# A fused transformer step on one core: three normalisations issued at other places or by another engine

## The chip, the cores and the metric

The kernel runs on 1 core of one Trainium2 chip. The metric is the device time of the program in microseconds; the time of a kernel is the median of its runs. Everything is computed in fp32.

In the profile the engines are PE (TensorE, matmuls), PEld (TensorE's weight loads), DVE (VectorE), ACT (ScalarE), POOL (GpSimd) and SP (SyncE, which only issues transfers here). Nearly all instructions are issued through a helper on line 50, so that "L50" says little; the names of the tiles, written as "out<-in", say which step a row is.

## What is computed

The input is a batch of 16 sequences `x` of 256 tokens by 256, and a context of 16 by 77 by 256. Four sublayers follow each other, each with a residual and a tanh gate:

```
x = x + tanh(g_xattn[0]) * attention0(ctx_1024, layernorm(x))   # 16 heads of 64, latents x attend to x and context
x = x + tanh(g_ffn[0])   * experts(layernorm(x))                # router softmax, best 2 of 8 experts per token
x = x + tanh(g_xattn[1]) * attention1(layernorm(x), ctx_1024)   # 16 heads of 16, 77 keys, mask, side factor
x = x + tanh(g_ffn[1])   * gated_linear_attention(layernorm(x))
```

In `attention0` the sequence is normalised twice: by the sublayer's own layer norm, and again inside. Each layer norm is `(x - mean) / sqrt(var + 1e-5)` over the 256 features of a token.

## The kernel before

The 16 batches are worked through stage by stage: stage 0 is the first attention, stage 1 the experts, stage 2 the second attention, stage 3 the gated linear attention. A token lies on a partition, so that a batch is 128 partitions by 2 rows of 256. The fast version of each stage (`stage0_fast`, `stage1_fast`, `stage2_fast`, `stage3_fast`) is the one that runs. A flag that is computed on the way would send the input through a slower version, which does not run here.

**What sets the order.** The engines run beside each other, each one through its own instructions in order, waiting on semaphores. Instructions issued through `dve`, `act`, `pool` and `pe` are kept in the order in which the program is written (line 160, class `Pinned`, line 42). Transfers through `nc.sync` (SP's queue) and `nc.gpsimd.memset` are not pinned; the framework orders those. Hand-written tables say which step of which batch is issued at which place.

**A layer norm** is made of three steps. `moments` (line 184) has DVE take the mean and variance of each token (tiles `bst`, `mv`). Then `rs` = 1/sqrt(var + eps) is computed either by POOL, with a multiply-add and a power (two instructions), or, with `by_act=True`, by ACT, with a logarithm and an exponential (two instructions). `normed` (line 200) multiplies -mean by `rs` on DVE (one instruction into `rs`) and then has ACT write the normalised rows (`y`, `xn`, `cn` or `rxn`), one activation per 256-wide row.

**Stage 0** works in 64 units, 16 batches by 4 groups of heads (loop at line 716). A unit issues the scores of four heads (`scores`, tile `sc`) with three exponentials on ACT (`e`), then on POOL the sums over keys (`sums`, tiles `es` and `esum`), then the values of the unit before (`values`, tiles `o`, `rd`), and the queries and keys of the next unit (`heads`, tile `qk`). Tables name what is issued ahead of a unit's scores (`ahead_of`, line 681), behind its scores (`behind_scores`, line 683) and behind its values, by the unit's group g. In them a batch's normalisation for the next batch is spread: statistics of `x` and context in group 3, `y` behind the scores of group 3, the second statistics ahead of the next group 0, and `normed_all`, which writes `xn` and `cn`, behind the scores of that group 0. In group 1 follow the transposes (`turn`), in group 2 the values' projection (`all_values`). The first batches are different: batch 0's norms stand in front of the loop, and batch 1's first three steps too (lines 711 to 713). Its second statistics and `normed_all(1)` come from the tables at unit 0.

In passing, stage 0 also routes batches for stage 1 (class `Route`, line 370 and after): norm, transposes, router logits, choice of two experts, weights, ranks, the places of the rows, and four scatters per batch, by which POOL writes weighted rows into DRAM (`rows`), sorted by expert. The last batches' routing steps lie in stage 1.

**Stage 1** runs 48 expert units (`units`, line 1125), two halves of 24, three units per expert and half (two, two and one tiles of 128 rows). In each round of the loop the next unit's transposes are issued first (`turned(u + 1)`, copied out by ACT into `xT`), then the unit's matmuls (`expert(u)`, tile `ex`, copied out by DVE into `y` and written to `rows_out` by SP), then the steps that the table `steps` (line 1110) has for this unit. The table places batch 15's routing (`last`): statistics in unit 1, norm in 2, and so on, to the four scatters in units 12 to 15. Expert rows are fetched by SP (`fetch`, tile `xin`). Rows of the second half need the last batch's scatters. Between the halves the context's keys and values for stage 2 are projected (`context`, tiles `k`, `kd`, `v`, `vc`). POOL gathers the experts' results back into `x` (`next_gather`, 64 transfers, 10 between the halves, 22 in the second half, the rest in stage 2). The mask's minimum and maximum per key are reduced by DVE (`mask`, tiles `mk`, `mm`).

**Stage 2** is a loop over batches (line 1270). In batch b the scores for two groups of heads are made one after the other into one PSUM tile (`sc`, of which there is one), each followed by an exponential on ACT (`e`); DVE multiplies by the side factor (`weigh`, tile `pg`), the matmuls `o` follow, ACT computes 1/denominator (`rd`), DVE the outputs (`oT`), and `project` updates `x`. Beside it the next batches are prepared by the class `Prepare` (line 1152): `turn` and `queries` of batch b + 1, `norm` of b + 2, `stats` of b + 3, and `spread` of b + 1, by which POOL copies the context's values into `vd`. `stats` is called behind `outputs(b, 0)`, so that DVE's statistics of b + 3 stand behind those of the outputs; the call that computes `rs` is behind them. Between these steps three gathers per batch are issued on POOL. Batches 0 to 2 have their `stats` in stage 1 (units 30, 35 and 40 of 48), batches 3 to 15 in stage 2. The line that decides who computes `rs` is

```
self.mv[b] = moments(xs[b], by_act=b < 5)
```

Of the kernel before, what the change touches and what calls it, by code (L numbers as in the profile page):

```python
# [73 lines left out]
def layers(ctx: ExitStack, tc: tile.TileContext, t, out, check):  # L74
# [11 lines left out]
    xs, cs = [None] * B, [None] * B  # L86
# [23 lines left out]
    def load_c(b):  # L110
        cs[b] = ctxs.tile([S2, D], F32, tag="c", name="c")
        nc.sync.dma_start(out=cs[b], in_=t["ctx"][b])
# [71 lines left out]
    def moments(src, p=P, n=2, by_act=False):  # L184
        mv = st.tile([P, 2, 2], F32, tag="mv", name="mv")
        rs = st.tile([P, 2, 2], F32, tag="rs", name="rs")
        bst = st.tile([P, 2, 6], F32, tag="bst", name="bst")
        for i in range(n):
            dve.bn_stats(bst[:p, i, :], src[:, i, :])
        for i in range(n):  # L190
            dve.bn_aggr(mv[:p, i, :], bst[:p, i, :])
        if by_act:
            act.activation(rs[:p, 0, :n], mv[:p, :n, 1], AF.Ln, bias=eps[:p])
            act.activation(rs[:p, 0, :n], rs[:p, 0, :n], AF.Exp, scale=-0.5)
            return mv, rs
        pool.tensor_scalar(rs[:p, 0, :n], mv[:p, :n, 1], 1.0, EPS, ALU.mult, ALU.add)
        pool.tensor_tensor(rs[:p, 0, :n], rs[:p, 0, :n], nhalf[:p, :n], ALU.pow)
        return mv, rs

    def normed(dst, src, mv, rs, p=P, n=2):  # L200
        dve.scalar_tensor_tensor(rs[:p, 1, :n], mv[:p, :n, 0], -1.0, rs[:p, 0, :n], ALU.mult, ALU.mult)
        for i in range(n):
            act.activation(dst[:, i, :], src[:, i, :], AF.Identity, bias=rs[:p, 1, i:i + 1],
                           scale=rs[:p, 0, i:i + 1])
# [165 lines left out]
    class Route:  # L370
# [11 lines left out]
        def stats(self, b):  # L382
            self.mv[b] = moments(xs[b])
# [132 lines left out]
    if fast:  # L516
        route = Route()
# [6 lines left out]
    def clear_rows():  # L524
        zero = ws1.tile([P, D], F32, tag="zero", name="zero")
        nc.gpsimd.memset(zero, 0.0)
        n = ROWS // P
        for rows in route.rows:
            for e in range(8):
                nc.sync.dma_start(out=by_expert(rows, e),  # L530
                                  in_=bc(zero, [P, n, D], 1))

    def stage0_fast():
        with ExitStack() as sx:
# [17 lines left out]
            def norm_c(b):  # L552
                mvs[b, "c"] = moments(cs[b].unsqueeze(1), S2, 1)

            def norm_x(b):
                mvs[b, "x"] = moments(xs[b])
# [4 lines left out]
            def normed_y(b):  # L561
                y[b] = w1.tile([P, 2, D], F32, tag="y", name="y")
                normed(y[b], xs[b], *mvs.pop((b, "x")))
# [39 lines left out]
            def heads(b, g, n):  # L603

                if n == 0:
                    qk[b, g] = w2.tile([P, 2, S + NK], F32, tag="qk", name="qk")
                m = 2 * g + n
                both = pair("qk")
                psq, psk = both[:, 0, :], both[:, 1, :]
                for k in range(2):  # L610
                    pe.matmul(psq[:, :S], wq0[:, k, m * P:(m + 1) * P], kvT[b][:, k, :S], start=k == 0, stop=k == 1)
                for k in range(2):
                    pe.matmul(psk[:, :NK], wkv0[:, k, m * P:(m + 1) * P], kvT[b][:, k, :], start=k == 0, stop=k == 1)
                act.mul(qk[b, g][:, n, :S], psq[:, :S], 0.125)
                dve.tensor_copy(qk[b, g][:, n, S:], psk[:, :NK])

            def scores(b, g):

                x_qk = qk.pop((b, g))
                e = w2.tile([KC, 6, 2, S], F32, tag="e", name="e")  # L620
                for u in range(0, 6, 2):
                    sc = pair("sc").rearrange("p j (x s) -> p j x s", x=2)
                    for x in range(2):
                        n, c = divmod(u + x, 3)
                        for j in range(2):
                            r = slice(64 * j, 64 * j + 64)
                            pe.matmul(sc[:KC, j, x, :], x_qk[r, n, S + c * KC:S + (c + 1) * KC],
                                             x_qk[r, n, :S], start=True, stop=True)
                    act.activation(e[:, u:u + 2], sc[:KC].rearrange("p j x s -> p x j s"), AF.Exp)
                return b, g, e  # L630

            def sums(b, g, e):
                es = w2.tile([KC, 2, 2 * S], F32, tag="es", name="es")
                by_chunk = e.rearrange("p (n c) j s -> p n c (j s)", n=2)
                pool.tensor_tensor(es, by_chunk[:, :, 0], by_chunk[:, :, 1], ALU.add)
                pool.tensor_tensor(es, es, by_chunk[:, :, 2], ALU.add)
                for n in range(2):
                    pool.tensor_tensor(esum[:KC], esum[:KC], es[:, n, :], ALU.add)
                return b, g, e, es
# [27 lines left out]
            def tally():  # L667
                for rd, to in tallies:
                    act.activation(rd, rd, AF.Identity, accum_out=to)
                tallies.clear()  # L670

            def project(b):
                both = pair("proj")
                for i in range(2):
                    for m in range(8):
# [5 lines left out]
            ahead_of = {0: [(norm_y, 1), (route.exps, -2)], 1: [(route.choose, -2)],  # L681
                        2: [(route.weigh, -2), (route.stats, -1)], 3: [(route.place, -2), (norm_x, 2), (norm_c, 2)]}
            behind_scores = {0: [(normed_all, 1), (route.scatter, -3, 1)],
                             1: [(route.scatter, -3, 2)],
                             2: [(route.norm, -1), (route.scatter, -3, 3)],
                             3: [(normed_y, 2), (route.scatter, -2, 0)]}
            behind_values = {2: [(route.ranks, -2, bank), (route.turn, -1, bank)], 3: [(route.logits, -1, bank)]}

            def run(steps, b, g):
                for f, d, *a in steps.get(g, ()):  # L690
                    if 0 <= b + d < B:
                        f(b + d, *a)
# [15 lines left out]
            all_values(0)  # L708
            heads(0, 0, 0)
            heads(0, 0, 1)  # L710
            norm_c(1)
            norm_x(1)
            normed_y(1)
            units = [(b, g) for b in range(B) for g in range(4)]
            behind = None
            for n, (b, g) in enumerate(units):
                ahead = units[n + 1] if n + 1 < len(units) else None
                run(ahead_of, b, g)
                now = scores(b, g)
                if g == 0 and b + 2 < B:  # L720
                    load_c(b + 2)
                run(behind_scores, b, g)
                if b == 0 and g == 1:
                    clear_rows()
                now = sums(*now)
                if behind is not None:
                    values(*behind)
                if g == 1 and b + 1 < B:
                    turn(b + 1)
                if g == 1 and b > 0:  # L730
                    project(b - 1)
                run(behind_values, b, g)
                if g == 2 and b + 1 < B:
                    all_values(b + 1, *route.weighted(b - 2))
                if ahead is not None:
                    heads(*ahead, 0)
                    heads(*ahead, 1)
                if g == 2 and b + 1 == B:
                    pieces = route.weighted(b - 2)
                    pieces[0]()  # L740
                if g == 3 and b + 1 == B:
                    pieces[1]()
                    pieces[2]()
                tally()
                behind = now
# [248 lines left out]
    def stage1_fast(keep, prep, bank):  # L994
        with ExitStack() as sx:
# [99 lines left out]
            last = B - 1  # L1095
# [9 lines left out]
            def weigh_rows(n):  # L1105
                if n == 0:
# [1 line left out]
                weighted[n]()  # L1108

            steps = {0: [(route.ranks, last - 1, bank)], 1: [(route.place, last - 1), (route.stats, last)],  # L1110
                     2: [(route.norm, last)], 4: [(route.turn, last, bank)], 5: [(route.logits, last, bank)],
                     6: [(route.exps, last)], 7: [(route.choose, last)], 8: [(route.weigh, last)],
                     9: [(route.ranks, last, bank), (weigh_rows, 0)], 10: [(weigh_rows, 1), (route.place, last)],
                     11: [(weigh_rows, 2)],
                     half + 6: [(prep.stats, 0)], half + 10: [(prep.norm, 0)], half + 11: [(prep.stats, 1)],
                     half + 13: [(prep.turn, 0)], half + 15: [(prep.norm, 1)], half + 16: [(prep.stats, 2)],
                     half + 17: [(prep.queries, 0)], half + 19: [(prep.turn, 1)], half + 20: [(prep.spread, 0)]}
            for n in range(4):
                steps.setdefault(2 + n, []).append((route.scatter, last - 1, n))
                steps.setdefault(12 + n, []).append((route.scatter, last, n))  # L1120
            for b in range(B):
                steps.setdefault(b, []).append((load, b))
                steps.setdefault(min(6 + b, half - 1), []).append((mask, b))
# [28 lines left out]
    class Prepare:  # L1152
# [11 lines left out]

        def stats(self, b):

            self.mv[b] = moments(xs[b], by_act=b < 5)

        def norm(self, b):
            self.xn[b] = self.pool.tile([P, 2, D], F32, tag="xn", name="xn")  # L1170
# [887 lines left out]
```

## Times and profile before

| what | us |
|---|---|
| median of 3 runs | 1944.18 |
| lowest and highest of them | 1939.99, 1945.24 |
| the profiled execution's own time | 1940.42 |
| its span | 1938.6 |
| busy: PE, DVE, POOL, ACT | 1902.5, 1089.7, 992.4, 871.8 |
| stage 0, about | 0 to 974 |
| stage 1, about | 974 to 1094 |
| stage 2, about | 1094 to 1250 |
| stage 3, about | 1250 to 1938 |

The mean granted clock of TensorE in the profiled execution is 0.996 of full speed.

How to read it: the profile is one execution, and times in it count from the start of its span. A row of the timeline gives the start, the length (of all merged instructions together), the engine, the line, the operation, the tiles, and in brackets how long the engine stood idle before it and what ended the wait. "PEq", "SPq" are the sequencers of these engines. The rows of DMA_INDIRECT on POOL are the scatters and gathers that it issues. A wait is put down to the last event that the profile saw, so a named engine that had long been done stands for another, often a transfer.

### The profile page before, as it was taken

The numbers are of one execution on the slowest core, as the hardware profiler recorded it, in microseconds if no ns is written. First come the engines' busy times: TensorE is split into PE (matmuls) and PEld (weight loads), VectorE is DVE, ScalarE is ACT, GpSimd is POOL, SyncE is SP. The second block draws the span as 40 slices with busy tenths as digits, with TensorE's granted clock in tenths as the row PEclk, the third lists the DMA queues.
The fourth block names the chain that finished last, engine by engine and source line by source line (L and its number), as shares of the span: only waits on it lengthen the run. The fifth ranks groups of instructions, "written<-read, shape, count | busy, mean of one in ns | idle before, by whom it ended". The sixth has DMA issues, their size and how long they took to land.

```text
span 1938.6 us, 34988 instructions
## 1 busy us (share of the span) xinstructions
PE 1902.5 (98%) x14028; PEld 1322.9 (68%) x14028; DVE 1089.7 (56%) x2637; ACT 871.8 (45%) x1807; POOL 992.4 (51%) x891
## 2 busy tenths in 40 slices
PE   8999999999999999999999899999999999999997
PEld 5666676666766666666687656667777777777775
DVE  3334555454554545554463478875666656666654
ACT  3333344433444344353333478744444444444442
POOL 4644757556675566655625736124444344444433
PEclk9999999999999999999999999999999999999999
DMA  9300000000000000000088723000000000000000
GB/s 342 133 1 3 14 11 14 10 10 11 12 13 11 9 11 12 9 9 10 14 270 244 183 32 48 11 1 6 7 7 6 12 6 7 6 6 7 12 7 13
DMA packets 54028, 75.03 MB, mean 39 GB/s; under 512 B 10097, under 2 KB 43745, under 8 KB 53345
## 3 DMA queue, kind: packets, MB, share of 16 engines
q1 hardware_dynamic: 41568, 55.92, 8.5%
q0 software_dynamic: 12288, 16.79, 4.3%
q8 instruction: 112, 1.84, 0.4%
q14 instruction: 60, 0.48, 0.1%
HBM read 39.14 MB, written 33.55 MB: 37 GB/s over the span
## 4 chain that ended last, share of the span: by engine, by line
PE 93%; DVE 2%; ACT 1%; DMA 1%; SPq 1%; issue 0%; POOL 0%; ACTq 0%; POOLq 0%; DVEq 0%
PE o L50 13%; PE qk L50 13%; PE sc L50 10%; PE v L50 9%; PE proj L50 7%; PE kq L1542 6%; PE sc L1542 5%; PE ex L50 3%; PE gq L1542 3%; PE v L1542 3%; PE proj L1542 3%; PE o L1542 3%; PE gz L1542 2%; PE z L1542 2%; PE den L1542 1%; PE q L50 1%
## 5 line engine op out<-in xcount | busy, mean ns | idle before, releaser
L50 POOL TENSOR_SCALAR rs<-mv 128x2 f32<-128x2 f32 (+1 forms) x90 | 17.3, 192 | 472.3 <-DVE mv L50 468.6
L50 ACT ACTIVATE qk<-qk 128x256 f32<-128x256 f32 x128 | 49.2, 385 | 341.3 <-PE qk L50 341.3
L50 ACT ACTIVATE e<-sc 111x1024 f32<-111x1024 f32 x192 | 182.3, 1021 | 17.0 <-PE sc L50 17.0
L50 PE MATMUL sc<-qk 64*111 64x256 f32 x1536 | 182.2, 383 | 1.8 <-DVE qk L50 1.8
L50 PE MATMUL o<-e,v 111*32 111x256 f32 x3072 | 177.5, 379 | 0.0
L50 PEld LDWEIGHTS sc<-qk 64*111 64x111 f32 x1536 | 132.1, 172 | 54.8 <-issue 28.5
L50 DVE RECIPROCAL rd<-o 128x256 f32<-128x256 f32 x64 | 112.3, 1755 | 101.1 <-PE o L50 101.1
L50 PE MATMUL v<-wkv,kvT 128*111 128x512 f32 x384 | 167.6, 593 | 0.6 <-DVE kvT L50 0.6
L50 POOL TENSOR_TENSOR esum<-esum,es 111x512 f32<-111x512 f32 x128 | 163.0, 1273 | 10.0
L50 PE MATMUL qk<-kvT,wkv 128*128 128x333 f32 x512 | 164.3, 443 | 0.0
L50 POOL TENSOR_TENSOR es<-e 111x1024 f32<-111x1024 f32 x64 | 151.3, 2365 | 25.1 <-ACT e L50 23.9
L50 POOL TENSOR_TENSOR k<-e,ee 128x256 f32<-128x256 f32 x64 | 47.0, 734 | 219.8 <-ACT e L50 219.8
L50 POOL TENSOR_TENSOR es<-es,e 111x1024 f32<-111x1024 f32 x64 | 150.4, 2351 | 5.0
L50 PEld LDWEIGHTS o<-e,v 111*32 111x32 f32 x3072 | 99.8, 110 | 65.9
L50 PE MATMUL qk<-kvT,wq 128*128 128x256 f32 x512 | 134.4, 385 | 0.9 <-ACT e L50 0.9
L50 DVE COPY qk<-qk 128x333 f32<-128x333 f32 x128 | 64.5, 505 | 125.5 <-ACT qk L50 124.0
L50 PEld LDWEIGHTS v<-wkv,kvT 128*111 128x111 f32 x384 | 66.5, 176 | 90.4 <-issue 89.0
L50 POOL TENSOR_TENSOR at<-at,at 128x768 f32<-128x768 f32 x63 | 114.0, 1810 | 24.9 <-DVE at L50 15.2
L50 DVE TENSOR_TENSOR at<-sc,amask 128x768 f32<-128x768 f32 x64 | 61.3, 958 | 115.8 <-PE sc L1542 100.5
L50 PEld LDWEIGHTS qk<-kvT,wq 128*128 128x128 f32 x512 | 94.3, 189 | 35.2 <-issue 13.2
L50 POOL DMA_INDIRECT x<-rows_out,pos x64 | 99.9, 1561 | 35.9 <-issue 16.2
L50 PEld LDWEIGHTS qk<-kvT,wkv 128*128 128x128 f32 x512 | 97.2, 190 | 30.0
(247 smaller groups left out, 4132.3 us busy)
## 6 DMA issues: line engine op xcount, KB each, us to landing
rows<-zero SPq DMA_DIRECT2D x16, 640.0 KB
xin<-rows SPq DMA_DIRECT2D x16, 640.0 KB
rows_out<-y SPq DMA_DIRECT2D x16, 384.0 KB
x<-in_x_dram SPq DMA_DIRECT2D x16, 256.0 KB
rows_out<-y SPq DMA_DIRECT2D x16, 256.0 KB
out_dram<-x SPq DMA_DIRECT2D x15, 256.0 KB
wkv<-in_wkv_dram SPq DMA_DIRECT2D x2, 1024.0 KB
ew<-in_ew_dram SPq DMA_DIRECT2D x2, 1024.0 KB
```

What stands on the lines that cost most here:

```text
L50: x = getattr(self.engine, name)(*a, **k)
L1542: tc.keep_in_program_order(nc.tensor.matmul(*a, **k))
```

## The change

Three parts, independent of each other.

1. In `stage0_fast` batch 1's first norm steps (`norm_c`, `norm_x`, `normed_y`) move from the place ahead of the loop to behind unit 0's scores and exponentials, followed there by its second statistics (`norm_y(1)`), which were ahead of unit 0's scores in program order. `normed_all(1)` moves from behind unit 0's scores to behind unit 1's. For all later batches the tables are as they were: for batch 0 the table entries of group 0 held nothing else, since the steps with batch numbers below 0 are left out.
2. In `stage1_fast` the last batch's norm moves from unit 2 to unit 3, and every routing step of that batch after it moves by one unit too, the four scatters from units 12 to 15 to units 13 to 16. The statistics stay in unit 1, the steps of the batch before stay where they are.
3. In `Prepare.stats` ACT computes `rs` for batches 0 to 2 only; for batches 3 and 4 POOL now does.

```diff
             heads(0, 0, 1)
-            norm_c(1)
-            norm_x(1)
-            normed_y(1)
             units = [(b, g) for b in range(B) for g in range(4)]
             behind = None
             for n, (b, g) in enumerate(units):
                 ahead = units[n + 1] if n + 1 < len(units) else None
-                run(ahead_of, b, g)
+                if n > 0:
+                    run(ahead_of, b, g)
                 now = scores(b, g)
                 if g == 0 and b + 2 < B:
                     load_c(b + 2)
-                run(behind_scores, b, g)
-                if b == 0 and g == 1:
+                if n == 0:
+
+                    norm_c(1)
+                    norm_x(1)
+                    normed_y(1)
+                    norm_y(1)
+                else:
+                    run(behind_scores, b, g)
+                if n == 1:
+                    normed_all(1)
                     clear_rows()
                 now = sums(*now)
...
             steps = {0: [(route.ranks, last - 1, bank)], 1: [(route.place, last - 1), (route.stats, last)],
-                     2: [(route.norm, last)], 4: [(route.turn, last, bank)], 5: [(route.logits, last, bank)],
-                     6: [(route.exps, last)], 7: [(route.choose, last)], 8: [(route.weigh, last)],
-                     9: [(route.ranks, last, bank), (weigh_rows, 0)], 10: [(weigh_rows, 1), (route.place, last)],
-                     11: [(weigh_rows, 2)],
+                     3: [(route.norm, last)], 5: [(route.turn, last, bank)], 6: [(route.logits, last, bank)],
+                     7: [(route.exps, last)], 8: [(route.choose, last)], 9: [(route.weigh, last)],
+                     10: [(route.ranks, last, bank), (weigh_rows, 0)], 11: [(weigh_rows, 1), (route.place, last)],
+                     12: [(weigh_rows, 2)],
...
             for n in range(4):
                 steps.setdefault(2 + n, []).append((route.scatter, last - 1, n))
-                steps.setdefault(12 + n, []).append((route.scatter, last, n))
+                steps.setdefault(13 + n, []).append((route.scatter, last, n))
...
         def stats(self, b):
 
-            self.mv[b] = moments(xs[b], by_act=b < 5)
+            self.mv[b] = moments(xs[b], by_act=b < 3)
```

## The prediction

> **What bounds the kernel now.** I read the page first, then the chain that ended last, then the timeline around the three places that the change touches, then the granted clock there.
>
> ```profile
> PE 1902.5 (98%) x14028; PEld 1322.9 (68%) x14028; DVE 1089.7 (56%) x2637; ACT 871.8 (45%) x1807; POOL 992.4 (51%) x891
> PE 93%; DVE 2%; ACT 1%; DMA 1%; SPq 1%; issue 0%; POOL 0%; ACTq 0%; POOLq 0%; DVEq 0%
> ```
>
> TensorE is busy 1902.5 of 1938.6 us. Work moved off another engine is worth nothing as such: only what removes one of TensorE's 36.1 us of gaps counts, or what raises its clock. So each edit is judged by the gap nearest to it.
>
> The start (waits stand in brackets at the end of a row):
>
> ```profile
> 27.10 2.85 PE L50 MATMUL sc<-qk 64*111 64x256 f32 x24
> 30.95 1.09 ACT L50 ACTIVATE y<-x,rs 128x256 f32<-128x256 f32 x2 [3.36 <-DVE rs L50]
> 31.95 2.83 ACT L50 ACTIVATE e<-sc 111x1024 f32<-111x1024 f32 x3
> 34.85 2.35 POOL L50 TENSOR_TENSOR es<-e 111x1024 f32<-111x1024 f32 x1 [1.01 <-ACT e L50]
> 37.10 2.85 PE L50 MATMUL sc<-qk 64*111 64x256 f32 x24 [1.84 <-DVE qk L50]
> 39.88 0.64 PE L50 MATMUL o<-es,ones 111*32 111x256 f32 x8
> ```
>
> The first scores start at 27.10, but their exponentials only at 31.95: batch 1's normalisation `y` stands ahead of them on ACT and waits for its statistics. TensorE pays 0.87 us (33.00, waiting for `e`) and 1.84 us (37.10).
>
> Stage 1, the experts' first half:
>
> ```profile
> 983.27 0.19 POOL L50 TENSOR_SCALAR rs<-mv 128x2 f32<-128x2 f32 x1 [0.56 <-DVE mv L50]
> 984.50 1.09 ACT L50 ACTIVATE rxn<-x,rs 128x256 f32<-128x256 f32 x2 [3.25 <-DVE rs L50]
> 985.50 0.83 ACT L50 COPY xT<-xT 128x512 f32<-128x512 f32 x2
> 986.11 1.99 PE L50 MATMUL ex<-ew,xT 128*128 128x256 f32 x8 [2.29 <-ACT xT L50]
> ```
>
> ACT stands 3.25 us at the last batch's `rxn`; the copy `xT` of expert unit 4, whose transposes ended at 981.88, is behind it, and TensorE stands 2.29 us.
>
> Stage 2, batches 1, 2 and then 3:
>
> ```profile
> 1108.92 0.30 ACT L50 ACTIVATE rs<-mv,eps 128x2 f32<-128x2 f32 x1 [2.29 <-DVE mv L50]
> 1111.45 1.10 PE L50 MATMUL sc<-qT,kd 32*77 32x256 f32 x16 [1.45 <-ACT e L50]
> 1121.35 0.30 ACT L50 ACTIVATE rs<-mv,eps 128x2 f32<-128x2 f32 x1 [2.29 <-DVE mv L50]
> 1123.88 1.50 PE L50 MATMUL sc<-qT,kd 32*77 32x256 f32 x16 [2.32 <-ACT e L50]
> 1135.55 0.19 POOL L50 TENSOR_SCALAR rs<-mv 128x2 f32<-128x2 f32 x1 [21.76 <-DVE mv L50]
> 1135.55 1.10 PE L50 MATMUL sc<-qT,kd 32*77 32x256 f32 x16
> ```
>
> Twice ACT stands 2.29 us at `rs` for DVE's statistics with the batch's exponential behind it, and TensorE stands 1.45 and 2.32 us for that exponential. From batch 5's statistics on, POOL computes `rs`, and the wait is gone. The windows below, one per batch from one first score matmul to the next, give it whole (length first, then busy us of PE, PEld, DVE, ACT, POOL, granted clock, DMA):
>
> ```profile
> 1105.60:1118.00 12.40, 10.96 (x118) 6.69 (x117) 8.27 (x15) 8.61 (x18) 7.11 (x7) 0.93 0.42 61
> 1118.00:1132.07 14.07, 11.75 (x121) 7.33 (x117) 9.21 (x16) 8.77 (x18) 0.00 (x0) 0.88 0.03 7
> 1132.07:1142.10 10.03, 10.03 (x120) 6.35 (x117) 8.47 (x15) 8.25 (x16) 5.81 (x7) 1.00 0.20 32
> ```
>
> Batches 1 and 2 take 12.40 and 14.07 us, batch 3 and its followers 10.03, TensorE full. Batch 2's 4.04 us of excess is 2.32 of wait and some 1.7 of matmuls at half clock (eight `q` 3.24 us instead of 1.99, sixteen `sc` 1.50 instead of 1.10).
>
> **What the Trainium skill says.** "TensorE: Matmul & The Clock Gate", section "What's actually happening": a free-running activity window of about 3.4 us sets TensorE to half clock after an idle window. The trace agrees: after the 2.32 us wait the granted clock is 0.50 from 1124.5 to 1127.2. The same page, "Architectural detail", calls ACT and DVE strict first-in first-out; the trace agrees, ACT idling 2.29 us at `rs` with the scores done. "ScalarE: Activation LUTs", "What ACT_TABLE_LOAD costs", gives 280 ns plus 0.833 ns per element for an activation with a pointer bias, 1.99 us for 2048; the trace has 1.95.
>
> **The change, part by part.**
>
> *Stage 2, batches 3 and 4's `rs` by POOL.* Removed from ACT: two times 0.30 + 0.20 us, and the two stands. Added on POOL: twice 0.19 + 0.72 us (rows at batch 5), about 1.0 with the gap between. In batch 1, the scores end near 1107.5; `e` starts there instead of at 1109.36, ends at 1109.65, and TensorE, which has its own work until 1110.0, goes straight on: the whole 1.45 us goes. The 0.86 us that batch 1 also loses (its first `sc` at half clock, 1.96 for 1.10) comes from an earlier gap, stays. Batch 2 becomes like batch 3: 14.07 - 10.03 = 4.04. Sum **5.5 us**; if the half-clock window comes without the wait, only 1.45 + 2.32 = 3.8.
> The added wait: POOL runs ahead here and is free at 1101.9; it will stand at batch 3's `rs` until DVE's `mv` at 1108.9. Behind it are queued a gather, `spread(1)` and the next batches' gathers. Batch 5's row shows the delay: from `rs` at 1135.55 to the end of the two `vd` copies at 1138.89 are 3.3 us, so `spread(1)` ends at 1112.3, and TensorE wants it at 1116.14 - 1.45 = 1114.7: hidden, 2.4 us to spare. The gathers lose their lead of about six, which batch 5's `rs` (POOL idle 21.76 us) takes away in any case. DVE wants `rs` itself at 1114, POOL has it at 1110. No loss.
>
> *Stage 1, the last batch's `norm` and what follows a unit later.* `xT` of unit 4 is copied at once (982.0 to 982.6), and unit 4's matmuls follow unit 3's at 983.8. `rxn` starts at about 984.6 as before, and now `xT` of unit 5 stands behind it: ready at 985.95, wanted at 986.1, after unit 4's 1.89 us. The 2.29 us go, up to 0.3 may return: **2.2 us**. Ten further steps move one unit (turn, logits, exps, choose, weigh, ranks, three weighings, place), with the same instructions, and four scatters. A unit is about as long as what is won, so in absolute time they stay. What is late next is that: the last scatter was issued at 1019.17, and the queue of SP stood 6.4 us for its landing, with a fetch at 1021.84, the last mask load (1022.29) and writes of results behind. DVE waits 4.53 us for that mask (1026.48) ahead of two evictions and the values' evictions (1028.27). TensorE, 2.2 us earlier, would find the first of these banks still full: key matmuls that came at 1029.40 could start at 1028.7 instead of 1027.2, a return of 1.5. SP's order isn't written by hand here; with the scatter a unit later I expect the mask load ahead of the waiting fetch, and the bank free. I take 2.2; ends 0.5 and 2.3.
>
> *Start, batch 1's norms behind the first exponentials.* Nothing is added; `e` can start 1.25 us after its scores (as at 68.17 to 69.42), at 28.35, and ends at 31.2. `y` follows at 31.1 (was 30.95), DVE's second statistics and POOL's `rs` end at 34.0, then POOL's sums `es` start at 34.05 instead of 34.85. TensorE loses both waits (0.87 + 1.84 - overlap: second scores at 35.35 instead of 37.10), but then waits for `es`, ready at 34.05 + 4.8 = 38.9, where it started the values at 39.88. So the gain is what POOL gains: **0.8 us**. `normed_all(1)` moves a unit, behind the second exponentials (end 39.45): 1.7 us of ACT, done at 41.1, wanted by the transposes at 42.2. Hidden, with 1.1 us to spare. Ends 0 and 1.75. No DMA moves: `load_c(2)` and the clearing keep their places in SP's queue.
>
> **Sum.** 5.5 + 2.2 + 0.8 = 8.5 us. The profiled execution took 1940.42 us (span 1938.6): it would take 1931.9. The median of the runs is 1944.18, 3.8 us above it, so I put the same sum on the median: **1935.7 us**.
>
> **Rivals.** *A, the waits go but are partly replaced* (SP's fetch still holds the mask load, stage 1 gives 0.7; the rest as above, 7.0): 1937.2. For it: the 6.4 and 4.53 us waits. Against: their order is free. *B, only bare waits return*: the half clock of batch 2 was one execution's phase of the window, or comes back elsewhere; 3.8 + 0.7 + 0.5 = 5.0: 1939.2, no measurable change. For it: the runs shown differ by 5.2 us among themselves. *C, POOL's queue becomes stage 2's bound, slower than before:* gathers of batch 0 wait for the experts' rows (2.49 us at 1098.46); if they, or those behind `rs`, wait longer, `spread(1)` and `spread(2)` are late for the values. It costs TensorE nothing up to the 2.4 us of spare time, then one for one; from 2.4 + 8.5 = 10.9 us of delay on it outweighs the whole gain. Three batches with 5 us each beyond the spare time would give 1944.18 - 8.5 + 15 = 1951. Against: POOL is busy 5.81 of 10.03 us in batch 3's window and then idles 3.09 us before the next `rs`. *D, more:* 2.02 us of wait at 1101.00 is followed by half clock until about 1107.5; shifted against the window, it may spare one: 1933.
>
> **Chances.** Forecast 0.53, A 0.17, B 0.18, C 0.05, D 0.07. About 0.3% (5.8 us) can be told from no change. Faster by more than that: forecast, A and D, less 0.07 that the scatter of the runs puts within: 0.70; within: B and these 0.07, 0.25; slower: C, 0.05. Range 1930 to 1941: D and the 2.6 us by which runs stray below, B and most of that above.
>
> **What would show it.** Right: no `rs` on ACT after 1095 and batch windows of about 11, 10 and 10 us with clock 1.00 in batch 2; no 2.29 us before `ex` in unit 4; `e` near 28.4 and the first `o` near 39.0. Wrong: a new wait of `k` or `v` matmuls on DVE's `vc` near 1027, of `o` on POOL's `vd` near 1114, of `ex` on unit 5's `xT`.

## The result and the profile after

The changed kernel took 1930.67 us (median of 5 runs, 1929.02 to 1932.43), the kernel before beside it 1940.71 (5 runs, 1939.99 to 1945.24). The ratio is 0.9941, with a 95% interval of 0.9926 to 0.9956. Below, a ratio is turned into microseconds with 1943 us, about what the kernel before took in the runs beside the experiments (medians 1943.91, 1942.77 and 1942.92). So the gain is 11.5 us (8.5 to 14.4); the medians differ by 10.0. The forecast was 8.5 us less, and 1935.7: the direction and the places were right, the size came out at about three quarters of the gain, and 1930.67 lies just inside the range of 1930 to 1941. (A "stand" below is time in which an engine waits idle with work queued.)

First the page of the changed kernel, busy time by engine and the chain that ended last:

```profile
PE 1901.3 (99%) x14028; PEld 1323.0 (69%) x14028; DVE 1091.0 (57%) x2637; ACT 870.4 (45%) x1803; POOL 993.5 (52%) x895
PE 95%; DVE 2%; ACT 1%; POOL 1%; issue 0%; DMA 0%; SPq 0%; ACTq 0%; POOLq 0%; DVEq 0%
```

TensorE's work is what it was (1901.3 us after 1902.5), the span is 1928.8 after 1938.6: its gaps shrank from 36.1 to 27.5 us. ACT has four instructions fewer and POOL four more, which are the two `rs`.

The start, from the changed kernel's timeline:

```profile
28.99 2.85 PE L50 MATMUL sc<-qk 64*111 64x256 f32 x24
30.15 2.85 ACT L50 ACTIVATE e<-sc 111x1024 f32<-111x1024 f32 x3 [0.67 <-PE sc L50]
...
32.88 1.10 ACT L50 ACTIVATE y<-x,rs 128x256 f32<-128x256 f32 x2
...
35.09 0.69 POOL L50 TENSOR_TENSOR rs<-rs,nhalf 128x2 f32<-128x2 f32 x1
35.74 2.36 POOL L50 TENSOR_TENSOR es<-e 111x1024 f32<-111x1024 f32 x1
...
35.93 2.85 PE L50 MATMUL sc<-qk 64*111 64x256 f32 x24
...
40.57 0.64 PE L50 MATMUL o<-es,ones 111*32 111x256 f32 x8 [1.80 <-POOL es L50]
```

The exponentials follow their scores at once and `y` comes behind them. The second scores start 6.94 us after the first instead of 10.00. But the values now stand 1.80 us for POOL's sums `es`, which start right behind POOL's `rs`. From the first scores to the first values it is 11.58 us, before 12.78: 1.20 won. (The first scores themselves came 1.89 us later than in the trace of before. The edit doesn't touch what lies ahead of them. Of the 14 traces of this study ten have 14.45 us from the first `v` matmul to these scores and four 16.2 to 16.4, with the start as before and as changed among both.)

Stage 1, the same view near unit 4:

```profile
983.97 0.19 POOL L50 TENSOR_SCALAR rs<-mv 128x2 f32<-128x2 f32 x1 [0.82 <-DVE mv L50]
...
984.36 1.89 PE L50 MATMUL ex<-ew,xT 128*128 128x256 f32 x8
985.19 1.09 ACT L50 ACTIVATE rxn<-x,rs 128x256 f32<-128x256 f32 x2 [1.94 <-DVE rs L50]
986.09 0.60 PE L50 MATMUL xT<-ident,xin 128*128 128x128 f32 x4
986.19 0.35 ACT L50 COPY xT<-xT 128x256 f32<-128x256 f32 x1
...
986.59 1.13 PE L50 MATMUL ex<-ew,xT 128*128 128x256 f32 x4
```

ACT still stands for `rs` (1.94 us), but unit 4's matmuls no longer do. They end at 986.25, and unit 5's start at 986.59, behind four transposes that stand between two units in any case. Unit 5's matmuls start 0.50 us behind the first transpose; ahead of unit 3 in the trace of before it was 0.44 (981.28 to 981.72). So less than 0.1 us returns here, and 0.54 in the trace of this part alone, below.

Stage 2, the windows of batches 0, 1 and 2 (columns as before):

```profile
1092.91:1101.40 8.49, 6.61 (x72) 3.62 (x73) 3.96 (x4) 6.12 (x9) 3.10 (x2) 1.00 0.51 122
1101.40:1111.43 10.03, 10.03 (x118) 6.36 (x116) 9.21 (x16) 8.22 (x16) 5.83 (x7) 1.00 0.30 46
1111.43:1121.47 10.04, 10.04 (x121) 6.36 (x117) 8.71 (x16) 8.24 (x16) 6.21 (x8) 1.00 0.32 48
```

Batches 1 and 2 are like all others, TensorE full at clock 1.00; they were 12.40 and 14.07. Batch 0, which no edit touches directly, fell from 11.00 to 8.49.

The sum over the two traces: first scores +1.9, start -1.2, stage 1 -2.4, batches 0 to 2 -8.9, all behind them +0.8; together -9.8. Read from one pair of executions, stage 1 seems right and stage 2 wrong. The experiments say otherwise.

### The profile page after: what moved, and what is told of

It is laid out like the page before. It is cut to its first block, busy times and chain, and to the rows that moved or that the text cites. A ratio compares the mean times of both kernels' runs of the same rounds, so it can differ in the third digit from the quotient of the medians.

```text
span 1928.8 us, 34998 instructions
## 1 busy us (share of the span) xinstructions
PE 1901.3 (99%) x14028; PEld 1323.0 (69%) x14028; DVE 1091.0 (57%) x2637; ACT 870.4 (45%) x1803; POOL 993.5 (52%) x895
## 4 chain that ended last, share of the span: by engine, by line
PE 95%; DVE 2%; ACT 1%; POOL 1%; issue 0%; DMA 0%; SPq 0%; ACTq 0%; POOLq 0%; DVEq 0%
PE o L50 13%; PE qk L50 13%; PE sc L50 10%; PE v L50 9%; PE proj L50 7%; PE kq L1548 6%; PE sc L1548 5%; PE ex L50 3%; PE gq L1548 3%; PE v L1548 3%; PE proj L1548 3%; PE o L1548 3%; PE gz L1548 2%; PE z L1548 2%; PE den L1548 1%; PE low L1548 1%
## 5 line engine op out<-in xcount | busy, mean ns | idle before, releaser
L50 POOL DMA_INDIRECT x<-rows_out,pos x64 | 100.1, 1564 | 37.3 <-issue 15.7
```

Source lines behind the costliest of these rows:

```text
L50: x = getattr(self.engine, name)(*a, **k)
```

## Experiments

### Each part alone, and the stands filled

`e1_start` is the first part of the diff alone, `e2_route` the second, `e3_pool_rs` the third. `e9_filled` is the kernel before with unread matmuls in the two stands of stage 2:

```diff
+                if b in (1, 2):
+                    ps = bank("warm")
+                    for _ in range(5 if b == 1 else 8):
+                        pe.matmul(ps[:, :D], ones, both[:, 1, :], start=True, stop=True)
                 run(scores, b, 1)
```

Expected of the start alone: 

> Part 1 alone (batch 1's norms behind unit 0's exponentials), the rest as before. Theory (each part acts by itself and the three add up): from the first scores of unit 0 to the first values matmul 11.6 us instead of 12.8, so about 1.2 us less in all and nothing in stages 1 and 2. Rival (the kernel's gain beyond the forecast is scatter between executions): 0 to 0.8 us here.

Expected of the routing alone: 

> Part 2 alone (the last batch's routing from its norm on a unit later). Theory: stage 1, from its first transposes to the first scores of stage 2, 117.7 us instead of 120.1; 2.4 us less, and the last mask load stands ahead of the fetch that waits for the scatters. Rival (only the wait moves): 0.7 us less, with a wait of the context matmuls for DVE near the middle of the stage.

Expected of stage 2's `rs` alone: 

> Part 3 alone (rs of batches 3 and 4 by POOL). Theory: batches 1 and 2 of stage 2 take 10.9 and 10.0 us instead of 12.4 and 14.1, 5.5 us less; the further 3.4 us that the changed kernel won in batches 0 and 1 are half-clock time and a faster first load, which are not of this edit and may or may not show. Rival (the edit also keeps the clock up in batches 0 and 1): 8 to 9 us less, in every execution.

Expected of the filled stands: 

> The kernel before, with 5 (batch 1) and 8 (batch 2) matmuls added, whose results nobody reads, where TensorE waits 1.45 and 2.32 us for the exponential; the waits for ACT stay. Theory (some 1.7 us of batch 2's excess is half clock that follows the idle time): the clock stays at 1.00 in batch 2, whose window is 12.3 us instead of 14.1, batch 1 at most 12.4; about 1.7 us less in all. Rival (the low clock has nothing to do with these waits): batch 2 stays at 14.1 us, no change.

| kernel | median, us | ratio to before (95%) | less than before, us |
|---|---|---|---|
| start alone | 1943.59 | 0.9995 (0.9981 to 1.0008) | 1.0 |
| routing alone | 1938.67 | 0.9974 (0.9965 to 0.9984) | 5.1 |
| stage 2 alone | 1938.85 | 0.9971 (0.9959 to 0.9983) | 5.6 |
| filled | 1943.36 | 0.9993 (0.9980 to 1.0006) | 1.4 |

The forecast had 0.8, 2.2 and 5.5 for the three parts. Stage 2 agrees, and the 8 to 9 us of its rival lie outside its interval (3.3 to 8.0). The routing gave more than twice its forecast; even the near end of its interval, 3.1 us, lies above the forecast's far end of 2.3.

What the trace of before had not shown is in that of stage 2 alone, whose stage 1 is as before:

```profile
984.38 0.96 POOL L50 DMA_INDIRECT rows<-xw,pos  x1 [3.71 <-DMA xin<-rows]
985.34 1.47 POOL L50 MEMSET vd<- 77x512 f32 x3
986.89 0.19 POOL L50 TENSOR_SCALAR rs<-mv 128x2 f32<-128x2 f32 x1
...
989.74 3.49 PE L50 MATMUL ex<-ew,xT 128*128 128x256 f32 x8 [4.59 <-ACT xT L50]
...
1037.06 2.34 PE L50 MATMUL k<-cT,wk 128*128 128x308 f32 x8 [1.54 <-DVE vc L50]
```

Three things come on top of the 2.29 us. POOL's `rs` stands behind a scatter that was issued late, so that TensorE stands 4.59 us. The eight `ex` after that take 3.49 us instead of 1.99, at half clock. And the key matmuls stand 1.54 us for DVE's `vc`, the stall that the prediction had named as late next.

The filled stands settle nothing: the ten and sixteen filling passes took longer than the 1.45 and 2.32 us that they were to fill:

```profile
1110.24 2.43 PE L50 MATMUL warm<-both,ones 128*128 128x256 f32 x10
...
1122.63 3.72 PE L50 MATMUL warm<-both,ones 128*128 128x256 f32 x16
```

Batch 2's window is 13.69 us at clock 1.00, about the 10.03 of a full batch and 3.72 of filling. That the filling kept the clock up isn't shown: of the six other traces with these two `rs` alone on ACT, three have batch 2 at clock 1.00 with the stand left empty (start alone, norm alone and masks alone, 12.42 or 12.43 us).

### The two stalls of stage 1 taken apart

Three variants of the kernel before: the norm alone a unit later, the masks reduced earlier (which puts the last mask load ahead of the waiting fetch in SP's queue), and both. All other routing steps and the scatters stay.

```diff
-                     2: [(route.norm, last)], 4: ...
+                     3: [(route.norm, last)], 4: ...
...
-                steps.setdefault(min(6 + b, half - 1), []).append((mask, b))
+                steps.setdefault(min(4 + b, half - 1), []).append((mask, b))
```

> The kernel before with the last batch's norm alone moved from unit 2 to unit 3; logits, choice, weights and scatters stay where they were, and the order of SP's queue keeps the fetch of the second half's rows ahead of the last mask load. My theory (two stalls in a row: ACT's stand at the normalisation, 2.3 us, and then TensorE's keys waiting for DVE behind the mask load, 0 to 1.5 us in the four profiles with this stage as before): TensorE comes 2.3 us earlier to the second stall, the scatters land when they landed, so up to 2 us are given back: 1.0 us less than the kernel before on the median (0 to 2), and a wait of the key matmuls for DVE of 1 to 3 us in the profile. Rival 1 (what counts in stage 1 is the half clock that follows the stand of 2.3 us, the mask costs nothing): 4 to 5 us less, all that the routing part gave. Rival 2 (the routing part is worth its 2.2 us and the rest of its 5.2 us was chance): 2.2 us less.

> The kernel before with the reduction of the masks two units earlier (unit 4 + b for batch b instead of 6 + b), so that the buffers come free earlier and the last mask load stands ahead of the waiting fetch in SP's queue; the norm stays in unit 2. My theory (the mask load behind the fetch costs TensorE 0 to 1.5 us by execution): 0.7 us less on the median, no wait of the key matmuls for DVE in the profile, and the wait of 2.3 us at unit 4 unchanged. Rival 1 (half clock) and rival 2 (chance): no difference.

> Both of the two edits above: the norm in unit 3, the masks reduced two units earlier, all other routing steps and the scatters as in the kernel before. My theory: neither stall is left, so this equals the whole routing part: 4 to 5 us less than before, and more than the two edits alone together, as the norm's gain is no longer given back. Rival 1: as the norm alone, 4 to 5. Rival 2: 2.2 us less. If it stays well below the routing part, the later scatters themselves have a share.

| kernel | median, us | ratio to before (95%) | less than before, us |
|---|---|---|---|
| norm alone | 1942.74 | 1.0000 (0.9989 to 1.0012) | 0.0 |
| masks alone | 1940.91 | 0.9992 (0.9978 to 1.0005) | 1.6 |
| both | 1939.32 | 0.9978 (0.9966 to 0.9989) | 4.3 |

Both together are worth about what the whole routing part is (4.3 against 5.1, intervals overlapping; by the medians 3.4 and 5.2), so the later scatters have no share that can be measured. The norm alone, which is what the 2.2 us had been forecast for, shows nothing, though its interval (2.1 us less to 2.3 more) still holds the 1.0 expected of it. Nor do these intervals tell 4.3 from the 1.6 of the two edits added up. That the second stall takes back a part of the first one's gain is seen in the trace of the norm alone (timelines of SP, DVE and TensorE):

```profile
1021.66 0.33 SPq L1068 DMA_DIRECT2D xin<-rows  x1
1022.10 0.32 SPq L1014 DMA_DIRECT2D mk<-in_maskT_dram  x1
...
1026.26 0.74 DVE L50 TENSOR_REDUCE mm<-mk 77x1 f32<-77x256 int32 x2 [6.30 <-DMA mk<-in_maskT_dram]
...
1028.51 2.34 PE L50 MATMUL k<-cT,wk 128*128 128x308 f32 x8 [0.94 <-DVE vc L50]
```

The wait ahead of unit 4 is gone there, but the fetch still waits for the last scatter's landing, the mask load for the fetch, DVE 6.30 us for the mask, and TensorE 0.94 us for DVE. (This execution was the fastest of its kernel's 14, 1936.58 us; how much is taken back in the others, the trace doesn't show.) With the masks early and the norm as before it is the other way round, the mask load at 1016.47 and the fetch at 1024.75, and unit 4 standing:

```profile
1016.47 0.31 SPq L1014 DMA_DIRECT2D mk<-in_maskT_dram  x1
1024.75 0.33 SPq L1068 DMA_DIRECT2D xin<-rows  x1
...
987.64 1.99 PE L50 MATMUL ex<-ew,xT 128*128 128x256 f32 x8 [2.28 <-ACT xT L50]
```

The Trainium skill, "DMA: Bandwidth & Descriptors", section "Anatomy of one DMA — SWDGE (gpsimd) path", says that any wait for a semaphore happens on the issuing sequencer before dispatch. The section is about POOL's transfers. The trace shows the same in SP's queue: the mask load, which needs nothing of the scatter, was issued 0.44 us behind the fetch that does.

The traces of all kernels, from stage 1's first transposes to stage 2's first scores (us), with TensorE's two stands:

| stage 1 | kernel | length | ahead of unit 4's `ex` | of the keys |
|---|---|---|---|---|
| as before | before | 120.13 | 2.29 | none |
| | start alone | 121.55 | 2.28 | 1.10 |
| | stage 2 alone | 126.56 | 4.59 | 1.54 |
| | filled | 121.03 | 2.35 | none |
| | rs of 8 by ACT (below) | 124.57 | 2.58 | 1.50 |
| | rs of 4 by POOL (below) | 124.01 | 2.44 | 1.15 |
| norm alone | | 119.62 | none | 0.94 |
| masks alone | | 120.10 | 2.28 | none |
| both | | 118.08 | none | none |
| as changed | five traces | 117.49 to 118.32 | none | none |

Of six executions with this stage as before, the profiled one of the prediction was the shortest. Their median is 122.8, that of the five with the stage as changed 117.86: 4.9 us apart, close to the 5.1 of the runs. In the three longest the matmuls behind unit 4's stand ran at half clock (3.49, 2.67 and 2.73 us for eight `ex` instead of 1.99). The changed stage also varies less: 0.8 us among five traces, after 6.4 among six.

### The changed kernel again, on the same chip as these

> The changed kernel once more, on the same chip as the edits above. If the parts add up (0.3 for the start, 5.2 for the routing, 5.1 for stage 2, each measured alone), 10.6 us less than before. If the gains of the parts share something (the half clock windows), 8 or less; if they help each other, more than 13.

1930.14 us (6 runs) against 1942.77, a ratio of 0.9937 (0.9918 to 0.9955): 12.2 us less. The three parts alone sum to 11.7. Within the intervals they add up; a few us that one part owes to another would not show in them.

### More and fewer stands in stage 2

The line that decides, in the kernel before, with 8 and with 4 in place of 5; and the changed kernel without `by_act` there, so that POOL computes the `rs` of batches 0 to 2 as well:

```diff
-            self.mv[b] = moments(xs[b], by_act=b < 5)
+            self.mv[b] = moments(xs[b], by_act=b < 8)
```

> The kernel before with ACT computing rs for three batches more in stage 2 (batches 5, 6 and 7 besides 3 and 4). My theory (each batch whose rs ACT computes in stage 2 makes ACT stand for DVE's statistics ahead of an exponential): three more windows of 12.4 to 14.1 us in place of 10.03, so 7 to 12 us more than the kernel before, 8.5 at the likeliest; the waits of the scores for e rise from two to five. Rival (POOL's own delay costs about as much as ACT's): under 3 us more. If the window of half clock comes with each stand, 12.

> The kernel before with rs of batch 4 alone given to POOL; batch 3's stays with ACT. My theory: the wait of 2.3 us in the window of batch 2 goes, that of batch 1 stays (0.9 to 1.5 us and its half clock): 2.4 us less than before without a half clock window behind the stand, 4 with it; 3 at the likeliest. Then batch 3's rs is the other 2 to 3 us of the 5.6 that both gave. Rival (the two stands share one half clock window, and only both edits together spare it): under 1.5 us less.

> The changed kernel with the rs of batches 0, 1 and 2 by POOL as well, where POOL issues gathers back to back in stage 1's second half. Rival C's mechanism (POOL's queue becomes the bound): batch 0's rs comes behind the 17th gather, three normalisations come late, 3 us or more slower than the changed kernel. My theory: by the gathers' times in the changed kernel's trace rs of batch 0 would be ready near 1064.6 and is wanted at 1067.0, that of batch 1 near 1074.5 and wanted at 1077.3; about 3 us of POOL work more in front of stage 2's gathers is hidden too: within 1 us of the changed kernel (1930.4), so 12 to 13 us less than before.

With three batches more on ACT: 1957.05 us, ratio 1.0067 (1.0052 to 1.0083), 13.0 us more. The windows of batches 3 to 5 in its trace:

```profile
1135.65:1151.10 15.45, 13.13 (x120) 8.21 (x116) 8.87 (x15) 8.78 (x18) 3.68 (x4) 0.78 0.14 23
1151.10:1165.21 14.11, 11.79 (x120) 7.59 (x117) 8.78 (x15) 8.67 (x18) 0.00 (x0) 0.88 0.03 7
1165.21:1179.28 14.07, 11.75 (x121) 7.30 (x117) 8.78 (x15) 8.74 (x18) 0.00 (x0) 0.88 0.03 7
```

They were 10.03 each; their excess is 13.5 us, the run's 13.0. TensorE stands 2.32 us in each and then works 1.7 to 3.1 us longer at clock 0.78 to 0.88. So a stand of 2.3 us costs 4.0 to 5.4 us here. The likeliest value that was expected, 8.5, was too low; the 12 that was named for half clock with every stand is near, and it came with every one. That ACT's order makes the stands is shown: three `rs` more on ACT, three stands more.

With batch 4 alone given to POOL: 1941.31 us, ratio 0.9989 (0.9980 to 0.9999), 2.1 us less. The window of batch 2 is 10.03 in the trace, that of batch 1 stays at 12.39. Its interval (0.2 to 3.9 us less) holds both the 3 that was expected and the rival's 1.5. By subtraction some 3.5 of the 5.6 us are batch 3's `rs`. With all on POOL: 1930.82 us, ratio 0.9934 (0.9918 to 0.9949), no different from the changed kernel. Its `rs` of batch 0 was ready at 1063.6, and ACT's `xn` started at 1066.40 (DVE took that `rs` at 1066.21), so that 2.6 us were left even among gathers issued back to back. Rival C's queue is not the bound.

### POOL's sums at the start

In the changed kernel batch 1's second `rs` goes to ACT:

```diff
                     normed_y(1)
-                    norm_y(1)
+                    mvs[1, "y"] = moments(y[1], by_act=True)
```

> The changed kernel with rs of batch 1's second statistics at the start by ACT in place of POOL, so that POOL's sums no longer stand behind it. My theory (part 1 gave only 1.2 us in the traces because POOL's sums es, ready to start at 33.0, stood for that rs until 35.7, and TensorE stood 1.80 us for them): the wait of 1.80 us goes, first scores to first values 9.8 to 10.1 us in place of 11.6; 1.5 us less than the changed kernel. Rival (the values then wait for something else, ACT's copies qk, which stand behind rs, above all): 0.5 us or less, with a new wait of the second scores.

```profile
30.88 2.36 POOL L50 TENSOR_TENSOR es<-e 111x1024 f32<-111x1024 f32 x1 [0.52 <-ACT e L50]
...
33.89 2.85 PE L50 MATMUL sc<-qk 64*111 64x256 f32 x24
...
36.66 0.64 PE L50 MATMUL o<-es,ones 111*32 111x256 f32 x8
```

The local claim holds: the sums start when `e` is ready, the wait of 1.80 us is gone, and from the first scores to the first values it is 9.87 us. The time, 1931.67 us (ratio 0.9935, 0.9919 to 0.9951), is not below the changed kernel's; the 1.5 us expected is less than the interval can tell (9.5 to 15.7 us less than before). In this execution stage 0 behind it was 1.7 us longer than in the changed kernel's traces, by a stretch at half clock:

```profile
166.00:170.00 4.00, 2.94 (x49) 1.72 (x41) 3.15 (x2) 1.14 (x3) 3.84 (x4) 1.00 0.00 0
170.00:174.00 4.00, 3.83 (x9) 1.68 (x9) 1.51 (x2) 0.94 (x3) 3.84 (x3) 0.66 0.00 0
```

That stretch follows the first batch's routing norm, where TensorE stands 1.06 us in all 14 traces. Three of them have the 1.7 us (this one, all on POOL, and masks alone), so it is not this edit's. Whether its 1.7 us of TensorE's time are ever seen in the total is left open; six runs don't tell.

## Why the prediction was right and wrong

**Start: right.** 0.8 us was forecast, 1.2 is in the traces and 1.0 (1.6 more to 3.7 less) in the runs. The reason was right too: what POOL gains is what TensorE gains. The last experiment shows it, where the wait for `es` goes together with POOL's `rs`.

**Stage 1: the step that failed.** The term of 2.2 us was too small by 2.9. "The 2.29 us go, up to 0.3 may return: 2.2 us" fits the one execution that it was read from; the runs gave 5.1 (3.1 to 7.0). The mechanism and the stall that comes next were named rightly, and so was the way out of it (the mask load ahead of the waiting fetch; in the changed kernel it is issued at 1015.53, the fetch at 1019.61). But the second stall was costed only as a possible return of 1.5 us on the gain. In fact it is paid with this stage as before in four of six traces, by 1.10 to 1.54 us, so that taking it away is a gain of its own. The trace of before even showed how near it was: DVE's `vc` at 1028.27, with key matmuls that came at 1029.40. Also left out was half clock behind the 2.29 us stand (three of six), though the same prediction counted it behind a stand of 2.32 us in stage 2. The upper end of 2.3 was therefore no bound.

**The base.** "The median of the runs is 1944.18, 3.8 us above it, so I put the same sum on the median." Stage 1 of that execution was 2.7 us shorter than the median of six (120.13, 122.8). That would be most of these 3.8 us, from the two things just named, which the changed kernel doesn't have. It isn't shown: the traced execution of the start alone took 1938.43 us with a longer stage 1 (121.55), and the median of three runs was itself loosely known (with two runs more it was 1940.71).

**Stage 2: right in its sum (5.5; 5.6 in the runs) by luck, as its parts were not.** Two errors stood against each other. Batch 1's other 0.86 us "stays" in three of the five traces with batches 3 and 4 on POOL (stage 2 alone 11.25, all on POOL 11.12, the last experiment 11.27) and is gone in both of the changed kernel itself (10.03). Batches 0 to 2 took 36.7 us on the mean of six traces with these two `rs` alone on ACT (the filled one left out), and 30.1 on that of the five with both on POOL: 6.6 won on the spot. But from the first scores of batch 15 to the end it was 681.8 to 682.7 us in the eight traces with batch 4's `rs` on ACT, and 683.5 to 684.9 in the six where it is on POOL: 2.1 us on the mean are given back. The windows of 3 us around the same place in stage 3 show it, first the norm alone, then the changed kernel again:

```profile
1276.99:1279.99 3.00, 2.11 (x12) 1.31 (x11) 3.00 (x5) 1.25 (x4) 0.73 (x1) 1.00 0.00 0
1279.99:1282.99 3.00, 2.98 (x14) 2.65 (x15) 1.11 (x4) 0.00 (x0) 1.42 (x2) 1.00 0.00 0
```

```profile
1267.52:1270.52 3.00, 3.00 (x12) 2.10 (x11) 3.00 (x5) 0.98 (x4) 0.73 (x1) 0.52 0.00 0
1270.52:1273.52 3.00, 3.00 (x9) 2.46 (x9) 1.12 (x4) 0.28 (x1) 1.42 (x2) 0.50 0.00 0
```

The work and the first small gaps (0.60 and 0.30 us) are the same, but in the second TensorE's clock is at a half. (In the kernel with batch 4 alone on POOL it falls some 11 us earlier, behind 3.41 us in which the trace shows no gap at all, 1263.42 to 1266.83.)

What differs is where this work falls in time against steps of the clock. In all 14 traces each stretch at half clock before the end of the kernel lasts 3.41 us, or twice or four times that, and the stretches of one trace start a whole number of such steps apart, in the last experiment at 171.27, 1099.70 and 1270.36, which are 272 and 50 steps. One stretch of the kernel before, with the steps around it:

```profile
1121.04:1124.45 3.41, 1.09 (x24) 0.50 (x20) 0.60 (x4) 3.07 (x6) 0.00 (x0) 1.00 0.00 0
1124.45:1127.86 3.41, 3.41 (x18) 2.23 (x11) 3.23 (x6) 3.00 (x6) 0.00 (x0) 0.50 0.08 23
1127.86:1131.27 3.41, 3.41 (x31) 2.46 (x34) 3.08 (x4) 1.81 (x4) 0.00 (x0) 1.00 0.00 0
```

(The prediction ended this stretch at 1127.2. Its 2.32 us of waiting are also shorter than the window of about 3.4 us that it says they agree with.) Counting such steps on through a trace, batch 15's first scores start 1.30 to 2.39 us behind the beginning of a step in the eight traces without half clock here, and 2.52 to 3.17 or 0.09 to 0.19 in the six with it. The 1.06 us stand of stage 0 begins 0.78 to 1.93 us behind one in the three traces with half clock there, and 1.99 to 3.30 or 0.21 to 0.42 in the eleven without. So whether the same work meets half clock goes with its place against these steps. No edit set that place on purpose, so this sorts the traces and is no experiment. Why all six traces with batch 4's `rs` on POOL came into the costly range of stage 3, and whether they must, was not tested.

**Sum.** 0.8 + 2.2 + 5.5 = 8.5 was forecast; the parts measured alone give 1.0 + 5.1 + 5.6 = 11.7, and the whole 12.2 (8.7 to 15.9). Of the 3.2 us between forecast and parts, 2.9 are stage 1's.

**Rivals.** A (the fetch still holds the mask load) is what the norm alone does, and shows 0.0 instead of the 0.7 forecast, with an interval that holds both; the change itself escapes it. B (only the bare waits) is refuted by the three more stands: 13.0 us for 7.0 of waits. It was right that batch 2's half clock depends on the execution: three of six traces with this stand have none. C (POOL's queue) did not appear, with five `rs` on it either. D (half clock in batch 0 and after it spared) happened in both traces of the changed kernel, whose batch 0 took 8.49 and 8.63 us; with stage 2 as before batch 0 took 8.68 to 11.00. But it took 9.35 to 10.69 in the three other traces with both `rs` on POOL, so it isn't shown to be the edit's.

## What to carry to other kernels

One execution shows a stand, not its spread: where a wait hangs on a transfer's landing, ask what it costs in an execution that is a microsecond less lucky, and where the median lies above the profiled time, look for the difference in such places before adding it to both kernels. Count half clock behind a stand of some 2 us as a chance: here it followed ten of 17 stands of 2.3 to 2.6 us in stages 1 and 2. Where two stalls come in a row, ask what the second takes back when the first is gone: here the first alone gave 0.0 us, the second 1.6, both 4.3, each by some 2 us either way.

## What the runs showed of the hardware

- Half clock came in steps of 3.41 us that ran on through the whole execution, and whether it followed a gap went with the place of the gap against these steps: the same 1.06 us stand was followed by half clock in three traces of 14, those in which it began 0.78 to 1.93 us into a step.
- A stand of TensorE of about 2.3 us cost 4.0 to 5.4 us in all three windows of the kernel with more stands, 2.4 in others (batch 2 with the start, the norm or the masks alone, 12.42 or 12.43 us). The difference is half clock.
- Much smaller gaps were followed by half clock as well: 0.60 and 0.30 us in stage 3, in five traces of 14 (in one of them with a third gap of 0.91), and 1.06 and 0.16 us in stage 0, in three of 14. In one trace it followed a step without any gap, so that idle time alone doesn't set it; what else counts, these runs don't show. The Trainium skill, "TensorE: Matmul & The Clock Gate", section "Why this matters for your kernels", asks for no idle gaps over about 3 us between bursts of matmuls; these runs show half clock below that, and the measurement decides.
- How long POOL stands ahead of a scatter varied between executions. Ahead of stage 1's first one it was 6.31 us in the trace of before and 7.96 in that of stage 2 alone, with the same instructions around it.
